# First attention's folded queries: contraction split 128 + 64 instead of 96 + 97 rows, with two heads' 64-row parts on the two halves of the array's rows

## Chip, cores and metric

One core of a Trainium2 chip. The time is the device time of one execution, in microseconds, as the median of the runs.

## What is computed

A post-norm decoder with two layers on x of 4 x 256 tokens and 512 features, all in float32. Each layer is attention, residual, layernorm, feed-forward, residual, layernorm. The change lies in the first layer's attention alone, 32 heads with low-rank queries and keys:

```python
q_c = hidden_size @ Wq_c.T + bq_c                      # 192 features
q = (q_c @ Wq_up.T + bq_up).reshape(b, s, NH, 192).transpose(0, 2, 1, 3)
kv = hidden_size @ Wkv_c.T + bkv_c                     # 64 latent + 64 rope
kv_nope, kv_rope = (kv[..., :64], kv[..., 64:])
kvu = (kv_nope @ Wkv_up.T + bkv_up).reshape(b, s, NH, 256).transpose(0, 2, 1, 3)
k_nope, v = (kvu[..., :128], kvu[..., 128:])
k = jnp.concatenate([k_nope, k_rope], axis=-1)         # k_rope: the same for all heads
scores = jnp.einsum('bhqd,bhkd->bhqk', q, k) / np.sqrt(192)
o = jnp.einsum('bhqk,bhkv->bhqv', softmax(scores), v)
out = jnp.einsum('bhsv,Hv->bsH', o, Wo) + bo           # one Wo for all heads
```

## The kernel before

The kernel never builds q and k of a head. Per head it multiplies the query weights with the key weights first ("the fold"), so that a folded query of 128 features (64 rope, 64 latent) meets the compressed keys kT (128 features x 1024 tokens), which all heads share. A scalar per token and head, beta, comes from the keys' bias; it moves the softmax's maximum. All of this runs before line 330; then come the feed-forward and the second layer, which the change doesn't touch.

The stages of the first attention, in program order:

1. **Projections** (L157 to L171). x transposed comes in four chunks on SyncE's DMA queue, the compressed weights wqc and wkvc on ScalarE's. TensorE makes qcT (192 query features, kept as two slabs of 96 rows, m = 0 and 1; slab 1 has a 97th row of ones, L154, which brings in the biases) and kT. VectorE adds the bias in the copy for qcT, ScalarE for kT. The other weights (wkn, eight groups wqn, the rope rows of wm, wvl, x, ...) follow on SyncE's queue, L138 to L150.
2. **The fold** (L174 to L188). Eight groups of four heads. For each slab m, four matmuls of query weights (96 or 97 columns) against 65 columns of key weights fill a bank ps_o; ScalarE copies slab 0 and VectorE slab 1 into wm, whose innermost index is the head: wm[:, m, :, h] is a strided read. A transpose of kT into cN follows in each group.
3. **First queries and beta** (L192 to L215). q_unit(h, hf) makes the folded queries of one head for 512 tokens: two matmuls (96 rows, then 97) into one bank ps_p, and one ScalarE copy with the scale into qh. Four of these for heads 0 and 1; then beta for eight token tiles, each two matmuls into a bank ps_p and a copy.
4. **The loop** (L298 to L315). j over 16 pairs of heads, b over 4 sequences, one pass for each (j, b). A pass issues scores0(j, b) (scores of two heads into two banks ps_s; maxima, nmb and ebias on VectorE; four exponentials on ScalarE), then, for the pass before, transposes0 (eight transposes into two banks ps_t, and two copies to pT0 and pT1, L269, both on VectorE), one q_unit for the next pair, in passes b = 2 and 3 of some pairs one value_unit (two matmuls into ps_p, added to oacc on VectorE), and output0 (four matmuls of 64 output columns, two heads on the two halves of a bank ps_o). Last, softmax0 normalises on VectorE.
5. **The end** (L316 to L324). The output projection and layernorm.

Banks of PSUM are handed out by tag, L54, with two each for p, s, t and o (L108): a third request of a tag waits until the first one has been read. The framework schedules the instructions at compile time: engines take them in its order, which is not always the order in the text. In the pass shown by the profile VectorE has the first pT copy ahead of nmb, which stands before it in the program.

A matmul of float32 operands is traced as two matmul instructions, each with a weight load of its own (PEld): 128 calls of L64 make 256 rows of ps_p<-qcT,wm.

The lines that decide about waits in the loop:

```python
if todo:
    q_unit(*todo.pop(0))
if flush and b >= 2:
    value_unit(*flush.pop(0))
if pending:
    output0(pending[0], pending[1], pTs)
```

Of the kernel before, what the change touches and what calls it, by code (L numbers as in the profile page):

```python
# [9 lines left out]
F32 = mybir.dt.float32  # L10
I32 = mybir.dt.int32
AF = mybir.ActivationFunctionType
ALU = mybir.AluOpType
# [13 lines left out]
RQ2 = RQ // 2  # L27
I = 1376
NI = -(-I // P)
NI2 = NI // 2  # L30
# [5 lines left out]
QSCALE = 1.0 / math.sqrt(DN + DR)  # L36
# [3 lines left out]
def tile_decoder2(ctx: ExitStack, tc: tile.TileContext, a: dict, out: bass.AP):  # L40
    nc = tc.nc
# [12 lines left out]
    def bank(tag, shape=(P, 512)):  # L54
        return ps["pool"].tile(list(shape), F32, tag=tag, name=f"ps_{tag}", bufs=ps["bufs"][tag])
# [6 lines left out]
    def mm(o, pairs):  # L62
        for i, (l, r) in enumerate(pairs):
            nc.tensor.matmul(o, l, r, start=(i == 0), stop=(i == len(pairs) - 1))  # L64
# [7 lines left out]
        out=mask, in_=mask, pattern=[[0, 2], [-1, P]], compare_op=ALU.is_ge,  # L72
# [4 lines left out]
    xT = const.tile([P, DC, N], F32, name="xT")  # L77
# [27 lines left out]
    NP = NH // 2  # L105
# [1 line left out]
    ps0 = ExitStack()  # L107
    ps0.enter_context(banks("ps0", p=2, s=2, t=2, o=2))  # L108
    with tc.tile_pool(name="l0", bufs=1) as l0, tc.tile_pool(name="l0b", bufs=2) as l0b:
        wkn = l0.tile([P, NH, RKV + 1], F32, name="wkn")  # L110

        wm = l0.tile([RQ2 + 1, 2, P + 1, NH], F32, name="wm")
        wqc = l0.tile([P, DC, RQ], F32, name="wqc")
        wkvc = l0.tile([P, DC, DR + RKV], F32, name="wkvc")
        cb = l0.tile([P, 3], F32, name="cb")
        wvl = l0.tile([P, NP, DV], F32, name="wvl")
        bv = l0.tile([P, NH], F32, name="bv")
        wo0 = l0.tile([P, D], F32, name="wo0")
        bo = l0.tile([P, D], F32, name="bo")
        qcT = l0.tile([RQ2 + 1, 2, N], F32, name="qcT")  # L120
        kT = l0.tile([P, N], F32, name="kT")
        cN = l0.tile([P, NT, RKV], F32, name="cN")

# [12 lines left out]
        nc.scalar.dma_start(out=cb[:RQ2, 0:2], in_=a["bqc"])  # L136
        nc.scalar.dma_start(out=cb[:, 2:3], in_=a["bkvc"])
        nc.sync.dma_start(out=wkn, in_=a["wkn"])  # L138
        wqns = [load_qn(g) for g in range(4)]
        nc.sync.dma_start(out=wm[:RQ2, 0, :DR, :], in_=a["wqr0"])  # L140
        nc.sync.dma_start(out=wm[:RQ2, 1, :DR, :], in_=a["wqr1"][:RQ2])
        nc.sync.dma_start(out=wm[RQ2:, 1, :DR, :], in_=a["wqr1"][RQ2:])
        wqns += [load_qn(g) for g in range(4, NG)]
        nc.sync.dma_start(out=wvl, in_=a["wvl"])
        nc.sync.dma_start(out=bv, in_=a["bv"])
# [4 lines left out]
        nc.sync.dma_start(out=usc, in_=a["usc"])  # L150

        nc.vector.memset(qcT[RQ2:RQ2 + 1, 1, :], 1.0)  # L154
        outs = []
        for hf, tags in enumerate(("pst", "pst")):
            for m in range(3):  # L157
                rows_m = P if m == 2 else RQ2
                outs.append((bank(tags[m]), hf, m, rows_m))
        for c in range(DC):  # L160
            for pj, hf, m, rows_m in outs:
                lhs = wkvc[:, c, :] if m == 2 else wqc[:, c, m * RQ2:(m + 1) * RQ2]
                nc.tensor.matmul(
                    pj[:rows_m], lhs, xT[:, c, bass.ts(hf, 512)], start=(c == 0), stop=(c == DC - 1)
                )
        for pj, hf, m, rows_m in outs:
            cols = bass.ts(hf, 512)
            if m == 2:
                nc.scalar.activation(kT[:, cols], pj, AF.Identity, bias=cb[:, 2:3])
            else:  # L170
                nc.vector.tensor_scalar(qcT[:RQ2, m, cols], pj[:RQ2], cb[:RQ2, m:m + 1], None, ALU.add)  # L171


        for g in range(NG):  # L174
            heads = slice(g * GH, (g + 1) * GH)
            for m in range(2):
                rows_m = RQ2 + m
                pj = bank("o", (P, GH, RKV + 1))
                for hh in range(GH):
                    mm(pj[:rows_m, hh, :], [  # L180
                        (wqns[g][:, hh, m * RQ2:m * RQ2 + rows_m], wkn[:, g * GH + hh, :])
                    ])
                copy = nc.scalar.copy if m == 0 else nc.vector.tensor_copy
                copy(wm[:rows_m, m, DR:, heads], pj[:rows_m].rearrange("p h c -> p c h"))

            tp = bank("t", (P, P))
            nc.tensor.transpose(tp, kT[:, bass.ts(g, P)], ident)
            nc.vector.tensor_copy(cN[:, g, :], tp[:, DR:])  # L188

        qh = {}  # L190

        def q_unit(h, hf):  # L192

            if h not in qh:
                qh[h] = l0b.tile([P, N], F32, tag=f"qh{h % 2}", name=f"qh{h}")
            cols = bass.ts(hf, 512)
            pj = bank("p")
            mm(pj, [
                (wm[:RQ2, 0, :P, h], qcT[:RQ2, 0, cols]),
                (wm[:, 1, :P, h], qcT[:, 1, cols]),  # L200
            ])
            nc.scalar.activation(qh[h][:, cols], pj, AF.Copy, scale=QSCALE)

        for u in [(h, hf) for h in range(2) for hf in range(2)]:
            q_unit(*u)

        beta = l0.tile([P, NT, NH], F32, name="beta")
        for t in range(NT):
            toks = bass.ts(t, P)
            pj = bank("p", (P, NH))  # L210
            mm(pj, [
                (qcT[:RQ2, 0, toks], wm[:RQ2, 0, P, :]),
                (qcT[:, 1, toks], wm[:, 1, P, :]),
            ])
            nc.scalar.activation(beta[:, t, :], pj, AF.Copy, scale=QSCALE)  # L215

        bvs = bv[:, 0:1]
        for n in (16, 8, 4, 2, 1):
# [40 lines left out]
        def transposes0(pr):  # L259
            pTs = []  # L260
            for i in range(2):
                tp = bank("t", (P, 2, S))
                for kt in range(2):
                    for qt in range(2):
                        nc.tensor.transpose(  # L265
                            tp[:, kt, qt * P:(qt + 1) * P], pr[:, i, qt, kt * P:(kt + 1) * P], ident
                        )
                pT = l0b.tile([P, 2, S], F32, tag=f"pT{i}", name=f"pT{i}")
                nc.vector.tensor_copy(pT, tp)  # L269
                pTs.append(pT)  # L270
            return pTs

# [47 lines left out]
        for t in range(NT):  # L320
            pj = bank("p")
# [20 lines left out]
    with tc.tile_pool(name="f0", bufs=1) as f0:  # L342
# [19 lines left out]
        with tc.tile_pool(name="f0i", bufs=2) as f0i, tc.tile_pool(name="f0w", bufs=3) as f0w:  # L362
# [82 lines left out]
            for c in range(NI2):  # L445
# [32 lines left out]
        with tc.tile_pool(name="f0d", bufs=2) as f0d:  # L478
# [78 lines left out]
    with banks("ps1", b0=1, b1=1, b2=1, s=2, t=2, o=1), \  # L557
# [291 lines left out]
        for j in range(NP):  # L849
# [15 lines left out]
            total, at, todo = sum(w for _, w in order), 0, {}  # L865
# [12 lines left out]
            for i in range(2 * B):  # L878
                h, b = (2 * j + i % 2, i // 2) if last else (2 * j + i // B, i % B)
# [5 lines left out]
                if pending:  # L885
                    pT = transposes1(pending[2])
# [11 lines left out]
def _layouts(i):  # L898
# [3 lines left out]
    def chunks(w):  # L902
        return w.reshape(-1, P, w.shape[1]).transpose(1, 0, 2)
# [8 lines left out]
    def columns(s):  # L912
# [3 lines left out]

    i = {k: np.asarray(v) for k, v in i.items()}
    x = i["L0_attn_hidden_size"].reshape(N, D)
    kvc = i["L0_attn_Wkv_c"]
    bkvc = i["L0_attn_bkv_c"]  # L920
# [7 lines left out]
    o = {  # L928
        "x": x.reshape(NT, P, D).transpose(1, 0, 2),
        "xT": chunks(x.T),  # L930
        "wqc": chunks(i["L0_attn_Wq_c"].T),
        "bqc": i["L0_attn_bq_c"].reshape(2, RQ2).T,
        "wkvc": chunks(np.concatenate([kvc[RKV:], kvc[:RKV]], axis=0).T),
        "bkvc": np.concatenate([bkvc[RKV:], bkvc[:RKV]])[:, None],
        "wqn": q[:, :DN].transpose(1, 0, 2),
        "wqr0": qr[:RQ2],
        "wqr1": qr[RQ2:],
        "wkn": kv[:, :DN].transpose(1, 0, 2),
        "wvl": kv[:, DN:, :RKV].reshape(NH // 2, 2, DV, RKV).transpose(1, 3, 0, 2).reshape(P, NH // 2, DV),
        "bv": kv[:, DN:, RKV].T,  # L940
        "wo0": i["L0_attn_Wo"].T,
# [36 lines left out]
```

## Time and profile before

| | us |
|---|---|
| median of 3 runs (lowest, highest) | 1759.63 (1758.41, 1761.05) |
| the profiled execution's own time | 1759.91 |
| its span in the trace | 1758.1 |
| first product of the projections | 4.46 |
| fold begins | 27.53 |
| first queries begin | 39.16 |
| beta and first scores begin | 46.14 |
| first output0 of the loop | 58.41 |
| last pass's output0 | 433.60 |

The granted TensorE clock was full throughout (mean 0.997). In the stretch from 104 to 416 us TensorE is busy for 312.0 of 312 us, VectorE for 220.4, ScalarE for 138.2, GpSimd for nothing, and there is no DMA to speak of. From 4 to 39 us the DMA engines are busy all the time.

How to read it: a row names line, engine, operation, output <- inputs and shape (for a matmul, rows*columns of the weights, then rows x columns of the moving operand). A timeline row gives start, length until the last end, and the number of instructions merged; in brackets the idle time of the engine before it and what ended it. Matmuls are pipelined and their lengths overlap, so start-to-start distances tell what they cost.

### The profile page before, as it was taken

The numbers are of one execution on the slowest core, as the hardware profiler recorded it, in microseconds if no ns is written. First come the engines' busy times: TensorE is split into PE (matmuls) and PEld (weight loads), VectorE is DVE, ScalarE is ACT, GpSimd is POOL, SyncE is SP. The second block draws the span as 40 slices with busy tenths as digits, with TensorE's granted clock in tenths as the row PEclk, the third lists the DMA queues.
The fourth block names the chain that finished last, engine by engine and source line by source line (L and its number), as shares of the span: only waits on it lengthen the run. The fifth ranks groups of instructions, "written<-read, shape, count | busy, mean of one in ns | idle before, by whom it ended". The sixth has DMA issues, their size and how long they took to land.

```text
span 1758.1 us, 20664 instructions
## 1 busy us (share of the span) xinstructions
PE 1722.8 (98%) x7352; PEld 1197.3 (68%) x7352; DVE 1063.8 (61%) x2528; ACT 486.6 (28%) x1584; POOL 478.4 (27%) x502
## 2 busy tenths in 40 slices
PE   8999999999899999999999999999999999999998
PEld 5766666665588885667667767766766776776543
DVE  1677777777745544556656566666656656667644
ACT  1444444444222101122222222222222222222433
POOL 0100000000456434222534335144325315332110
PEclk9999999999999999999999999999999999999999
DMA  8000000000521000101001011011001011010000
GB/s 279 1 1 1 1 1 1 1 1 1 177 70 49 1 1 12 48 25 43 31 24 49 24 36 37 25 36 48 25 24 54 19 49 36 19 48 21 29 12 25
DMA packets 30986, 60.85 MB, mean 35 GB/s; under 512 B 2690, under 2 KB 20354, under 8 KB 29154
## 3 DMA queue, kind: packets, MB, share of 16 engines
q1 hardware_dynamic: 29474, 58.86, 10.6%
q8 instruction: 59, 0.97, 0.2%
q10 hardware_dynamic: 1408, 0.66, 0.1%
q14 instruction: 45, 0.36, 0.1%
HBM read 57.41 MB, written 2.10 MB: 34 GB/s over the span
## 4 chain that ended last, share of the span: by engine, by line
PE 92%; DVE 5%; issue 1%; ACT 1%; DMA 0%; POOL 0%; ACTq 0%; DVEq 0%
PE ps_b L633 20%; PE ps_s L64 12%; PE ps_b L658 11%; PE ps_b L708 9%; PE ps_p L64 9%; PE ps_b L64 4%; PE ps_o L282 4%; PE ps_o L790 3%; PE ps_t L265 3%; PE ps_s L419 3%; PE ps_o L64 3%; PE ps_t L779 2%; PE ps_o L419 2%; PE ps_p L419 2%; PE ps_o L791 2%; DVE pr L773 1%
## 5 line engine op out<-in xcount | busy, mean ns | idle before, releaser
L792 ACT COPY att<-ps_o 128x256 f32<-128x256 f32 x128 | 47.6, 372 | 512.6 <-PE ps_o L791 512.5
L243 ACT ACTIVATE pr<-ps_s,ebias 128x256 f32<-128x256 f32 x256 | 117.7, 471 | 202.6 <-DVE ebias L238 202.6
L763 ACT ACTIVATE pr<-ps_s,nmx 128x128 f32<-128x128 f32 (+1 forms) x256 | 105.4, 417 | 142.2 <-DVE nmx L759 141.4
L716 DVE TENSOR_TENSOR x<-ps_b,x 128x512 f32<-128x512 f32 x168 | 114.9, 687 | 39.3 <-PE ps_b L708 28.9
L726 POOL TENSOR_TENSOR x<-x,po 128x512 f32<-128x512 f32 x84 | 104.8, 1269 | 106.6 <-DVE x L716 78.2
L64 PE MATMUL ps_s<-kT,qh 128*128 128x256 f32 x512 | 130.8, 393 | 0.6 <-ACT pr L243 0.2
L64 PE MATMUL ps_p<-qcT,wm 96*128 96x512 f32 (+1 forms) x256 | 126.5, 618 | 0.0
L373 POOL CAST fwg<-wiwg 128x512 f32<-128x512 int32 (+1 forms) x12 | 7.4, 648 | 403.2 <-DVE st L85 394.2
L64 PEld LDWEIGHTS ps_s<-kT,qh 128*128 128x128 f32 x512 | 90.0, 190 | 35.8 <-ACT pr L243 20.2
L773 DVE TENSOR_SCALAR pr<-pr,rc 128x128 f32<-128x128 f32 (+1 forms) x256 | 110.1, 462 | 4.2
L232 DVE TENSOR_REDUCE nmx<-ps_s 128x2 f32<-128x512 f32 x128 | 88.2, 689 | 37.7 <-PE ps_s L64 35.3
L64 PE MATMUL ps_s<-ck,cq 128*128 128x128 f32 (+1 forms) x512 | 105.2, 328 | 0.0
L755 DVE TENSOR_TENSOR ps_s<-ps_s,mask 128x256 f32<-128x256 f32 x128 | 55.4, 432 | 66.3 <-PE ps_s L64 63.3
L269 DVE COPY pT<-ps_t 128x512 f32<-128x512 f32 x128 | 86.6, 683 | 0.0
L790 PE MATMUL ps_o<-pT,v 128*128 128x256 f32 x256 | 77.4, 384 | 6.5 <-DVE pT L781 4.1
L64 PEld LDWEIGHTS ps_p<-qcT,wm 96*128 96x128 f32 (+1 forms) x256 | 70.9, 299 | 17.6
L759 DVE TENSOR_REDUCE nmx<-ps_s 128x1 f32<-128x128 f32 (+1 forms) x256 | 79.9, 353 | 4.3
L708 PE MATMUL ps_b<-ct,co 128*128 128x256 f32 x336 | 81.9, 380 | 0.0
L254 DVE TENSOR_SCALAR pr<-pr,rc 128x256 f32<-128x256 f32 x256 | 79.1, 349 | 3.1
L779 PEld LDWEIGHTS ps_t<-ident,pr 128*128 128x128 f32 x384 | 49.8, 141 | 41.6 <-issue 34.1
L781 DVE COPY pT<-ps_t 128x384 f32<-128x384 f32 x128 | 70.1, 547 | 12.4 <-PE ps_t L779 12.4
L790 PEld LDWEIGHTS ps_o<-pT,v 128*128 128x128 f32 x256 | 47.4, 190 | 43.3 <-issue 36.0
(248 smaller groups left out, 3559.2 us busy)
## 6 DMA issues: line engine op xcount, KB each, us to landing
w_wa<-in_wq SPq DMA_DIRECT2D x16, 512.0 KB, 3.9
w_wb<-in_wk SPq DMA_DIRECT2D x16, 512.0 KB, 3.9
w_wc<-in_wv SPq DMA_DIRECT2D x8, 1024.0 KB, 5.0
w_wd<-in_wo SPq DMA_DIRECT2D x16, 512.0 KB, 3.8
wqn<-in_wqn SPq DMA_DIRECT2D x8, 386.0 KB, 12.2
wiwg<-in_wg SPq DMA_DIRECT2D x5, 512.0 KB, 3.7
wiwu<-in_wu SPq DMA_DIRECT2D x5, 512.0 KB, 3.6
wid<-in_wd SPq DMA_DIRECT2D x10, 256.0 KB, 2.6
```

Of the source, the lines that this page charges most:

```text
L64: nc.tensor.matmul(o, l, r, start=(i == 0), stop=(i == len(pairs) - 1))
L232: nc.vector.tensor_reduce(nmx[:, i, :], sc, AX.X, ALU.max, negate=True)
L243: nc.scalar.activation(pr[:, i, qt, :], sc[:, qt, :], AF.Exp, bias=bias[:, i, qt:qt + 1], accum_out=sm[:, i, qt:qt + 1],)
L419: nc.tensor.matmul(banks_of[tag], lhs[i][:, k, :], rhs[i][:, k, :], start=first and k == 0, stop=k == 1, skip_group_check=True,)
L633: nc.tensor.matmul(acc, lhs[i][:, k, :], right[i][:, k, :], start=first and k == 0, stop=k == 1, skip_group_check=True,)
L658: nc.tensor.matmul(acc[:, tt, :], right[i][:, k, (t0 + tt) * P:(t0 + tt + 1) * P], lhs[i][:, k, :], start=first and tt == 0 and k == 0, st ...
L708: nc.tensor.matmul(st[tag][:, tt, :], lhs[i][:, (t0 + tt) * P:(t0 + tt + 1) * P], rhs[i], start=first and tt == 0, stop=True, skip_group_c ...
L716: nc.vector.tensor_tensor(xb[m][k], acc, xb[m][k], ALU.add)
L726: nc.gpsimd.tensor_tensor(xb[m][k], xb[m][k], st["p1"], ALU.add)
L763: nc.scalar.activation(pr[:, pt, :], sc[:, pt, :], AF.Exp, bias=nmx[:, qt:qt + 1], accum_out=sm[:, qt:qt + 1],)
L773: nc.vector.tensor_scalar(pr[:, pt, :], pr[:, pt, :], rc[:, qt:qt + 1], None, ALU.mult)
L790: nc.tensor.matmul(po, v[g][:, 2 * b, hv], pT[:, 0:2, :], start=True, stop=False)
```

## The change

The 192 query features are kept as 128 + 64. Slab 0 of qcT holds features 0 to 127; slab 1 holds features 128 to 191 twice, in rows 0 to 63 and again in rows 64 to 127 (wqc has 256 columns now, bqc 128 rows). The folded weights are two tiles: wma, 128 rows for each head, and wmb, whose rows 0 to 63 are the even head's and 64 to 127 the odd head's part, by pairs. The fold fills wmb with matmuls of 64 output columns, the two heads of a pair on the two halves of a bank. The biases are no longer a row of the contraction: the fold makes them in 32 matmuls of 65 weight columns and one moving column (bank pb), and ScalarE adds them, scaled, in the copy out of PSUM (qb). Beta gets a third matmul of one row (crow) and a layout of its own for the 64 rows (wmc, zeros for the other head); all tiles share one bank and one copy, and beta now stands ahead of the first queries.

In the loop, one pass (b = 0, 2) issues the 128-row products of both heads into the two banks ps_p; the next (b = 1, 3) issues the 64-row products, one head on rows 0 to 63 and one on 64 to 127, and then both copies. The second pT copy goes to ScalarE. Value products go to b = 1 and 3 instead of 2 and 3.

```diff
-        wm = l0.tile([RQ2 + 1, 2, P + 1, NH], F32, name="wm")
-        wqc = l0.tile([P, DC, RQ], F32, name="wqc")
+        wma = l0.tile([P, P + 1, NH], F32, name="wma")
+        wmb = l0.tile([P, P + 1, NP], F32, name="wmb")
+        wmc = l0.tile([P, NP, 2], F32, name="wmc")
+        qb = l0.tile([P, NH], F32, name="qb")
+        crow = l0.tile([P, NH + P], F32, name="crow")
+        wqc = l0.tile([P, DC, 2 * P], F32, name="wqc")
...
-        nc.sync.dma_start(out=wm[:RQ2, 0, :DR, :], in_=a["wqr0"])
-        nc.sync.dma_start(out=wm[:RQ2, 1, :DR, :], in_=a["wqr1"][:RQ2])
-        nc.sync.dma_start(out=wm[RQ2:, 1, :DR, :], in_=a["wqr1"][RQ2:])
+        nc.sync.dma_start(out=wma[:, RKV + 1:, :], in_=a["wqra"])
+        nc.sync.dma_start(out=wmb[:, RKV + 1:, :], in_=a["wqrb"])
+        nc.scalar.dma_start(out=qb[RKV:, :], in_=a["bqr"])
...
-        nc.vector.memset(qcT[RQ2:RQ2 + 1, 1, :], 1.0)
+        nc.gpsimd.memset(wmc, 0.0)
+        nc.gpsimd.memset(crow[RKV:RKV + 1, NH:], 1.0)
...
+        pb = bank("p", (P, NH))
         for g in range(NG):
-            heads = slice(g * GH, (g + 1) * GH)
-            for m in range(2):
-                rows_m = RQ2 + m
-                pj = bank("o", (P, GH, RKV + 1))
-                for hh in range(GH):
-                    mm(pj[:rows_m, hh, :], [
-                        (wqns[g][:, hh, m * RQ2:m * RQ2 + rows_m], wkn[:, g * GH + hh, :])
-                    ])
-                copy = nc.scalar.copy if m == 0 else nc.vector.tensor_copy
-                copy(wm[:rows_m, m, DR:, heads], pj[:rows_m].rearrange("p h c -> p c h"))
+            pja = bank("o", (P, GH, RKV + 1))
+            for hh in range(GH):
+                mm(pja[:, hh, :], [(wqns[g][:, hh, :P], wkn[:, g * GH + hh, :RKV + 1])])
+            nc.scalar.copy(wma[:, :RKV + 1, g * GH:(g + 1) * GH], pja.rearrange("p h c -> p c h"))
+            pjb = bank("o", (P, GH // 2, RKV + 1))
+            for hh in range(GH):
+                half = slice((hh % 2) * RKV, (hh % 2 + 1) * RKV)
+                mm(pjb[half, hh // 2, :], [(wqns[g][:, hh, P:RQ], wkn[:, g * GH + hh, :RKV + 1])])
+            pairs = slice(g * GH // 2, (g + 1) * GH // 2)
+            nc.vector.tensor_copy(wmb[:, :RKV + 1, pairs], pjb.rearrange("p h c -> p c h"))
+            for hh in range(GH):
+                h = g * GH + hh
+                mm(pb[:RKV + 1, h:h + 1], [(wkn[:, h, 1:], wqns[g][:, hh, RQ:])])
...
+        for n in range(2):
+            half = slice(n * RKV, (n + 1) * RKV)
+            nc.vector.tensor_copy(wmc[half, :, n], wmb[half, 0, :])
+        nc.scalar.activation(qb[:RKV], pb[:RKV], AF.Copy, scale=QSCALE)
+        nc.scalar.copy(crow[RKV:RKV + 1, :NH], pb[RKV:RKV + 1, :])
+        nc.vector.tensor_scalar(qb[RKV:], qb[RKV:], QSCALE, None, ALU.mult)
...
+        def q_units(j):
...
+            def upper(hf):
+                for n, h in enumerate(heads):
+                    if hf == 0:
+                        qh[h] = l0b.tile([P, N], F32, tag=f"qh{n}", name=f"qh{h}")
+                    acc[n] = bank("p")
+                    nc.tensor.matmul(
+                        acc[n], wma[:, 1:, h], qcT[:, 0, bass.ts(hf, 512)], start=True, stop=False,
+                    )
+
+            def lower(hf):
+                cols = bass.ts(hf, 512)
+                for n, h in enumerate(heads):
+                    half = slice(n * RKV, (n + 1) * RKV)
+                    nc.tensor.matmul(
+                        acc[n], wmb[half, 1:, j], qcT[half, 1, cols], start=False, stop=True,
+                    )
+                for n, h in enumerate(heads):
+                    nc.scalar.activation(
+                        qh[h][:, cols], acc[n], AF.Identity, bias=qb[:, h:h + 1], scale=QSCALE
+                    )
+
+            return [lambda hf=hf, part=part: part(hf) for hf in range(2) for part in (upper, lower)]
...
+        pj = bank("o", (P, NT, NH))
         for t in range(NT):
             toks = bass.ts(t, P)
-            pj = bank("p", (P, NH))
-            mm(pj, [
-                (qcT[:RQ2, 0, toks], wm[:RQ2, 0, P, :]),
-                (qcT[:, 1, toks], wm[:, 1, P, :]),
+            mm(pj[:, t, :], [
+                (qcT[:, 0, toks], wma[:, 0, :]),
+                (qcT[:, 1, toks], wmc.rearrange("p j n -> p (j n)")),
+                (crow[RKV:RKV + 1, NH:], crow[RKV:RKV + 1, :NH]),
             ])
-            nc.scalar.activation(beta[:, t, :], pj, AF.Copy, scale=QSCALE)
+        nc.scalar.activation(beta, pj, AF.Copy, scale=QSCALE)
+        for u in q_units(0):
+            u()
...
-                nc.vector.tensor_copy(pT, tp)
+                (nc.scalar.copy if i else nc.vector.tensor_copy)(pT, tp)
...
-            todo = [(h, hf) for h in (2 * j + 2, 2 * j + 3) for hf in range(2)] if j + 1 < NP else []
+            todo = q_units(j + 1)
...
                 if todo:
-                    q_unit(*todo.pop(0))
-                if flush and b >= 2:
+                    todo.pop(0)()
+                if flush and b % 2:
                     value_unit(*flush.pop(0))
```

More of the change, by code (lines that the diff above doesn't have):

```diff
@@ L26 @@
 RQ, RKV = 192, 64
-RQ2 = RQ // 2
 I = 1376
@@ L109, in tile_decoder2 @@
     with tc.tile_pool(name="l0", bufs=1) as l0, tc.tile_pool(name="l0b", bufs=2) as l0b:
-        wkn = l0.tile([P, NH, RKV + 1], F32, name="wkn")
-        wm = l0.tile([RQ2 + 1, 2, P + 1, NH], F32, name="wm")
-        wqc = l0.tile([P, DC, RQ], F32, name="wqc")
+        wkn = l0.tile([P, NH, RKV + 2], F32, name="wkn")
+        wma = l0.tile([P, P + 1, NH], F32, name="wma")
[4 more added lines that the diff above has]
+        wqc = l0.tile([P, DC, 2 * P], F32, name="wqc")
         wkvc = l0.tile([P, DC, DR + RKV], F32, name="wkvc")
@@ L119, in tile_decoder2 @@
         bo = l0.tile([P, D], F32, name="bo")
-        qcT = l0.tile([RQ2 + 1, 2, N], F32, name="qcT")
+        qcT = l0.tile([P, 2, N], F32, name="qcT")
         kT = l0.tile([P, N], F32, name="kT")
@@ L135, in tile_decoder2 @@
                 nc.sync.dma_start(out=xT[:, c, cols], in_=a["xT"][:, c, cols])
-        nc.scalar.dma_start(out=cb[:RQ2, 0:2], in_=a["bqc"])
+        nc.scalar.dma_start(out=cb[:, 0:2], in_=a["bqc"])
         nc.scalar.dma_start(out=cb[:, 2:3], in_=a["bkvc"])
@@ L150, in tile_decoder2 @@
         nc.sync.dma_start(out=usc, in_=a["usc"])
-        nc.vector.memset(qcT[RQ2:RQ2 + 1, 1, :], 1.0)
[L155 to L159, printed above, removed]
-        for c in range(DC):
[L161 to L166, printed above, removed]
+        nc.gpsimd.memset(wmc, 0.0)
+        nc.gpsimd.memset(crow[RKV:RKV + 1, NH:], 1.0)
+        outs = [(bank("pst"[m]), hf, m) for hf in range(2) for m in range(3)]
+        for c in range(DC):
+            for pj, hf, m in outs:
+                lhs = wkvc[:, c, :] if m == 2 else wqc[:, c, m * P:(m + 1) * P]
+                nc.tensor.matmul(pj, lhs, xT[:, c, bass.ts(hf, 512)], start=(c == 0), stop=(c == DC - 1))
+        for pj, hf, m in outs:
             cols = bass.ts(hf, 512)
@@ L170, in tile_decoder2 @@
             else:
-                nc.vector.tensor_scalar(qcT[:RQ2, m, cols], pj[:RQ2], cb[:RQ2, m:m + 1], None, ALU.add)
+                nc.vector.tensor_scalar(qcT[:, m, cols], pj, cb[:, m:m + 1], None, ALU.add)
+        pb = bank("p", (P, NH))
         for g in range(NG):
-            heads = slice(g * GH, (g + 1) * GH)
-            for m in range(2):
-                rows_m = RQ2 + m
-                pj = bank("o", (P, GH, RKV + 1))
-                for hh in range(GH):
-                    mm(pj[:rows_m, hh, :], [
-                        (wqns[g][:, hh, m * RQ2:m * RQ2 + rows_m], wkn[:, g * GH + hh, :])
-                    ])
-                copy = nc.scalar.copy if m == 0 else nc.vector.tensor_copy
-                copy(wm[:rows_m, m, DR:, heads], pj[:rows_m].rearrange("p h c -> p c h"))
+            pja = bank("o", (P, GH, RKV + 1))
[11 more added lines that the diff above has]
+                mm(pb[:RKV + 1, h:h + 1], [(wkn[:, h, 1:], wqns[g][:, hh, RQ:])])
@@ L186, in tile_decoder2 @@
             tp = bank("t", (P, P))
             nc.tensor.transpose(tp, kT[:, bass.ts(g, P)], ident)
-            nc.vector.tensor_copy(cN[:, g, :], tp[:, DR:])
-        qh = {}
[L192 to L197, printed above, removed]
-            mm(pj, [
[L199 to L202, printed above, removed]
@@ L204, in tile_decoder2 @@
-        for u in [(h, hf) for h in range(2) for hf in range(2)]:
-            q_unit(*u)
+            nc.vector.tensor_copy(cN[:, g, :], tp[:, :RKV])
+        for n in range(2):
[4 more added lines that the diff above has]
+        nc.vector.tensor_scalar(qb[RKV:], qb[RKV:], QSCALE, None, ALU.mult)
@@ new lines, in tile_decoder2 @@
+        qh = {}
+        def q_units(j):
+            if j >= NP:
+                return []
+            heads = (2 * j, 2 * j + 1)
+            acc = {}
+            def upper(hf):
[18 more added lines that the diff above has]
+            return [lambda hf=hf, part=part: part(hf) for hf in range(2) for part in (upper, lower)]
@@ L207, in tile_decoder2 @@
         beta = l0.tile([P, NT, NH], F32, name="beta")
+        pj = bank("o", (P, NT, NH))
         for t in range(NT):
             toks = bass.ts(t, P)
-            pj = bank("p", (P, NH))
-            mm(pj, [
-                (qcT[:RQ2, 0, toks], wm[:RQ2, 0, P, :]),
-                (qcT[:, 1, toks], wm[:, 1, P, :]),
-            ])
-            nc.scalar.activation(beta[:, t, :], pj, AF.Copy, scale=QSCALE)
+            mm(pj[:, t, :], [
+                (qcT[:, 0, toks], wma[:, 0, :]),
+                (qcT[:, 1, toks], wmc.rearrange("p j n -> p (j n)")),
+                (crow[RKV:RKV + 1, NH:], crow[RKV:RKV + 1, :NH]),
+            ])
@@ L918, in _layouts @@
     x = i["L0_attn_hidden_size"].reshape(N, D)
-    kvc = i["L0_attn_Wkv_c"]
-    bkvc = i["L0_attn_bkv_c"]
+    wqc = i["L0_attn_Wq_c"]
+    bqc = i["L0_attn_bq_c"]
     q = np.concatenate([i["L0_attn_Wq_up"], i["L0_attn_bq_up"][:, None]], axis=1)
@@ L930, in _layouts @@
         "xT": chunks(x.T),
[L931 to L934, printed above, removed]
+        "wqc": chunks(np.concatenate([wqc, wqc[P:]], axis=0).T),
+        "bqc": np.concatenate([bqc, bqc[P:]]).reshape(2, P).T,
+        "wkvc": chunks(i["L0_attn_Wkv_c"].T),
+        "bkvc": i["L0_attn_bkv_c"][:, None],
         "wqn": q[:, :DN].transpose(1, 0, 2),
-        "wqr0": qr[:RQ2],
-        "wqr1": qr[RQ2:],
-        "wkn": kv[:, :DN].transpose(1, 0, 2),
+        "wqra": qr[:P],
+        "wqrb": np.concatenate([qr[P:RQ, :, 0::2], qr[P:RQ, :, 1::2]], axis=0),
+        "bqr": qr[RQ],
+        "wkn": np.concatenate([kv[:, :DN, RKV:], kv[:, :DN]], axis=2).transpose(1, 0, 2),
         "wvl": kv[:, DN:, :RKV].reshape(NH // 2, 2, DV, RKV).transpose(1, 3, 0, 2).reshape(P, NH // 2, DV),
```

## The prediction

> **What bounds the kernel now.** First the page: TensorE has no idle time to speak of, and it carries the chain that ends last. The products that the change rewrites are the ps_p row, 256 instructions of one pass each.
>
> ```profile
> PE 1722.8 (98%) x7352; PEld 1197.3 (68%) x7352; DVE 1063.8 (61%) x2528; ACT 486.6 (28%) x1584; POOL 478.4 (27%) x502
> ...
> PE 92%; DVE 5%; issue 1%; ACT 1%; DMA 0%; POOL 0%; ACTq 0%; DVEq 0%
> ...
> L64 PE MATMUL ps_p<-qcT,wm 96*128 96x512 f32 (+1 forms) x256 | 126.5, 618 | 0.0
> ```
>
> Then TensorE's timeline over one pass of the inner loop (start, length, then the instructions merged). Lengths overlap, so I read starts.
>
> ```profile
> 171.89 1.99 PE L64 MATMUL ps_p<-qcT,wm 96*128 96x512 f32 x4
> 173.80 1.08 PE L282 MATMUL ps_o<-pT,cN 128*64 128x256 f32 x8
> 174.82 2.00 PE L64 MATMUL ps_s<-kT,qh 128*128 128x256 f32 x8
> 176.65 1.04 PE L265 MATMUL ps_t<-ident,pr 128*128 128x128 f32 x8
> 177.52 0.70 PE L64 MATMUL ps_p<-qcT,wm 96*128 96x512 f32 x1
> ```
>
> Start to start: queries 1.91, output 1.02, scores 1.83, transposes 0.87, together 5.63 us. Eight score instructions of 256 columns need 2.00 - 0.38 (length of the last) = 1.62 for seven steps, so one step is about 0.215 us, and 0.43 for 512 columns. In the output row eight instructions lie within 1.08: 1.08 - 0.38 = 0.70 is three steps. So they start two at a time, from the first: 64-column products on two halves of the array run together.
>
> Third, DVE and ACT over the same pass, and the end of the loop, where no queries are left to compute:
>
> ```profile
> 171.83 0.68 DVE L269 COPY pT<-ps_t 128x512 f32<-128x512 f32 x1
> 172.42 0.15 DVE L236 TENSOR_TENSOR nmb<-nmx,beta 128x4 f32<-128x4 f32 x1
> 172.49 0.69 DVE L269 COPY pT<-ps_t 128x512 f32<-128x512 f32 x1
> 173.09 0.16 DVE L238 TENSOR_TENSOR ebias<-nmb,beta 128x4 f32<-128x4 f32 x1
> ```
>
> ```profile
> 422.58 1.61 PE L282 MATMUL ps_o<-pT,cN 128*64 128x256 f32 x8
> 427.95 1.75 PE L282 MATMUL ps_o<-pT,cN 128*64 128x256 f32 x8 [0.65 <-DVE pT L269]
> ```
>
> ```profile
> 173.37 0.47 ACT L243 ACTIVATE pr<-ps_s,ebias 128x256 f32<-128x256 f32 x1 [3.69 <-DVE ebias L238]
> ```
>
> The exponentials wait for ebias, and ebias sits behind the second pT copy. There the period is 427.95 - 422.58 = 5.37: the loop through DVE and ACT. So a pass is bound by TensorE (5.63) with the softmax loop 0.26 behind it. Shorter queries alone would gain little; ACT's 3.69 idle is room for a copy.
>
> **The change part by part, against the profiled execution** (span 1758.1; its own time 1759.91; the median of the runs is 1759.63, 0.3 less).
>
> *Queries in the loop.* For two heads and 512 tokens there were 8 instructions in two passes of the loop, 4 and 4. Now the even pass has 4 with 128 rows (same 0.43 steps: no change), the odd pass has 4 of 64 rows, two for each half. If halves of the rows pair as halves of the columns do, these are two steps, 0.86. To this comes the change of tile mode. The Trainium skill (TensorEngine Tiling, Tiling Modes, Key Properties) says that changing the mode drains TensorE, which speaks against this change; it gives no time. The trace does: the four query steps from 171.89 end at 171.89 + 0.10 (first weights) + 4 x 0.43 = 173.71, and the output starts at 173.80, 0.09 late; and its first weights, no longer loaded ahead, add 0.05. Here the weights are 128 columns:
>
> ```profile
> L64 PEld LDWEIGHTS ps_s<-kT,qh 128*128 128x128 f32 x512 | 90.0, 190 | 35.8 <-ACT pr L243 20.2 <-issue 5.4
> L64 PEld LDWEIGHTS ps_p<-qcT,wm 96*128 96x128 f32 x128 | 33.3, 305 | 0.8
> L282 PEld LDWEIGHTS ps_o<-pT,cN 128*64 128x64 f32 x512 | 32.0, 136 | 55.5 <-DVE ebias L238 29.6 <-DVE pr L254 6.1 <-DVE rc L252 5.3
> ```
>
> From 64 to 128 packed columns a load grows 54 ns, 0.85 a column; strided by heads (305) it is about 115 more, some 0.22 us exposed. So the odd pass is 0.09 + 0.22 + 0.86 + 0.09 (drain before the output) = 1.26 instead of 1.91: 0.65 less. By the rule without the row I would have no number; with no drain it would be 1.05 less. 15 pairs of heads x 2 = 30 such passes: -19.6.
>
> What is late next? With the second pT copy on ACT, ebias follows nmb at once, 0.6 earlier, so the softmax loop is about 4.8, under the odd pass's 5.63 - 0.65 = 4.98. Its copy (about 0.6, by the 606 ns eviction of the same size) falls in ACT's 3.69 idle and costs nothing; with that cover gone it would delay four exponentials. ACT's two evictions in the odd pass (1.2 instead of 0.6) have the same cover. The last pair of heads, bound by the softmax loop at 5.37, gains 0.5 in four passes: -2.0.
>
> *Value products* go to odd passes, behind the lower products. Both ps_p banks then wait for ACT's evictions, which queue behind the four exponentials; behind the value product on TensorE are the output and the next scores. 14 places. Between nothing (the scheduler puts output and the first scores ahead) and 1.25 (the value product first: output done 1.0 after the lower products, bank free some 2.3 after). The trace shows work that is ready put ahead of work that isn't (the pT copy before nmb), so I take 0.15: +2.
>
> *Fold.* A group takes 28.98 - 27.53 = 1.45 now, of it 0.11 the transpose, so 0.084 for each of 16 loads of 96 columns:
>
> ```profile
> 27.53 1.50 PE L64 MATMUL ps_o<-wkn,wqn 128*96 128x65 f32 x16
> 28.87 0.28 PE L187 MATMUL ps_t<-ident,kT 128*128 128x128 f32 x1
> 28.98 1.50 PE L64 MATMUL ps_o<-wkn,wqn 128*96 128x65 f32 x16
> ```
>
> After: 8 loads of 128 columns at 0.111 = 0.89; 8 on column halves, four steps of 0.06, with 0.14 in and 0.16 out = 0.54; 8 for the bias, 65 weight columns for one moving column. For these the skill's floor per matmul (TensorE: Matmul & The Clock Gate, Back-to-back issue gap: about 25 ns however few columns) would give 0.2; but the row says that loads set the pace, 0.058 each: 0.41. Transpose 0.11. Sum 1.95, +0.5 x 8 = +4.0 (3 to 6).
>
> *Beta.* Per token tile 4 instructions of 0.111, now 2 more with one row, in another tile mode: 0.09 + 0.21 + 0.10 out = +0.40, x 8 = +3.2 (0.22 x 8 = 1.8 with no drain, 4.5 with the longer loads). Beta also goes ahead of the queries, so the first softmax no longer has beta products to cover it: a bubble of about +0.9 (scores' end to first bank free 2.7, covered by 1.8 of queries). The first pair's queries save 2 x 0.65: -1.3.
>
> *At nothing:* memsets, the small copies and the qb load (beside the fold's TensorE work; uncovered under 0.5 each); the loads behind wqn, whose issue order on SP stays. The 0.13 MB more of wqc delay the first product by about +0.1.
>
> Sum: -19.6 - 2.0 + 2.0 + 4.0 + 3.2 + 0.9 - 1.3 + 0.1 = -12.7. 1759.63 - 12.7 = **1747**.
>
> **Rivals.**
> - *Row halves start in strict order.* The skill (same page, Part 3, What overlaps and what doesn't) says that matmuls start in order. If both passes of a head stand before the other head's, three steps instead of two: 0.43 back in 32 places, +13.8: about 1760.5. The output row speaks against it (three steps to the last start, not four), but those are column halves; no row of the trace shows row halves.
> - *Row halves don't overlap at all* (slower). Four steps: +0.86 x 32 = +27.5: 1774.5. It decides from the point where the overlap saves less than 14.8 / 32 = 0.46 of the 0.86 per place, for without it the change costs 1774.5 - 1759.6 = 14.8. For it: no row of the trace has products on row halves. Against: column halves pair from the first step, and the two heads write different banks.
> - *Overlap as forecast, but the moved waits bite:* value products stall 1.25 in 14 places (+15.5 beyond mine), or the ACT copy lands behind the exponentials in some passes: about 1762. Against: ready work is put ahead.
>
> **How the numbers follow.** Forecast 0.54 (own range 1739 to 1754: fold and beta at their bounds, value stalls 0 to 6, and the 0.12 by which 22 passes run at 5.75 instead of 5.63, -2.6 if they even out); strict order 0.14; no overlap 0.17; waits 0.15. A measurement tells 0.2%, 3.5 us, from no change: faster is below 1756.1, slower above 1763.2. Faster: 0.54, 0.02 of strict order and 0.03 of waits: 0.59. Same: 0.10 of strict order and 0.03 of waits: 0.13. Slower: the rest, 0.28. The range 1739 to 1774 leaves out half of no overlap and the far ends of the others.
>
> **What would show it.** Right: the four 64-row instructions start two at a time, so that their row in the timeline is about 0.43 long to the last start; even passes 5.63, odd about 5.0; pT's second copy ahead of the exponentials on ACT; fold groups near 1.95. Wrong: the same row at 0.86 or 1.3 to the last start; TensorE waiting for ACT qh in odd passes; odd passes over 5.4.

## The result, and the profile after

| | before | after |
|---|---|---|
| median of 5 runs (lowest, highest) | 1759.63 (1758.41, 1761.05) | 1771.89 (1765.65, 1773.13) |
| ratio, with its 95% interval | | 1.0057 (1.0035 to 1.008) |
| span of the profiled execution | 1758.1 | 1771.3 |
| fold begins | 27.53 | 27.49 |
| first scores begin | 46.51 | 75.18 |
| first output0 of the loop | 58.41 | 83.94 |
| first product of the output projection | 435.14 | 445.85 |
| second layer's first product | 673.99 | 686.66 |

The kernel became slower, by 12 us; the forecast was 13 us faster. Of its five runs three took 1771.9 to 1773.1 us, with a mean clock of 0.984, and two 1765.7 us, with 0.988 and 0.989; the profile is that of the longest. The loop did get faster: from the first output0 to the output projection it took 376.7 us and takes 361.9, 14.8 less. All of that and more had been lost ahead of it: the loop starts 25.5 us late. The page of the changed kernel, with the lines that answer to those shown of before and the row of the clock:

```profile
PE 1733.0 (98%) x7432; PEld 1201.1 (68%) x7432; DVE 1033.5 (58%) x2466; ACT 531.5 (30%) x1643; POOL 478.5 (27%) x504
...
PEclk8699999999999999999999999999999999999999
...
PE 90%; DVE 6%; ACT 2%; issue 1%; DMA 0%; POOL 0%; ACTq 0%; DVEq 0%
```

TensorE is as busy as it was, and the chain is still its own. What is new are two digits: in the first two fortieths of the span (to 44 and to 89 us) the granted clock was 0.8 and 0.6. In the kernel before that row has a 9 in every place. (Its clock was not full quite throughout: from 671.49 to 678.32 us, after an idle stretch between the two layers, it was half, and every kernel here has such a dip.) The same by stretches (length, then busy time and instructions of each engine, the granted clock, the DMA share and GB/s):

```profile
core 0: us, PE busy (x) PEld busy (x) DVE busy (x) ACT busy (x) POOL busy (x), PEclk, DMA share, GB/s
...
27.00:32.77 5.77, 5.77 (x69) 5.19 (x68) 1.84 (x6) 1.44 (x3) 0.00 (x0) 1.00 1.06 432
32.77:49.00 16.23, 16.23 (x119) 15.16 (x118) 2.30 (x9) 2.16 (x7) 10.84 (x13) 0.50 0.26 99
49.00:55.00 6.00, 6.00 (x26) 3.93 (x25) 0.93 (x4) 0.47 (x2) 0.00 (x0) 0.50 0.00 0
55.00:68.00 13.00, 13.00 (x51) 11.62 (x51) 0.00 (x0) 0.28 (x1) 0.00 (x0) 0.50 0.00 0
```

From 32.77 to 73.73 us, that is in nearly all of the fold, in beta and in the first queries, TensorE ran at half clock, although from 32.77 to 49.00 us it was busy for 16.23 of 16.23 us, and before the drop for 5.77 of 5.77. A fold group takes 3.85 us there and a token tile of beta 1.55. Then the clock is full again, and the loop shows the mechanism that was forecast. TensorE's timeline over an odd pass and the start of one with a value product:

```profile
175.69 1.04 PE L295 MATMUL ps_t<-ident,pr 128*128 128x128 f32 x8
176.66 1.23 PE L223 MATMUL ps_p<-qcT,wmb 64*128 64x512 f32 x4
177.82 1.08 PE L312 MATMUL ps_o<-pT,cN 128*64 128x256 f32 x8
178.84 1.13 PE L63 MATMUL ps_s<-kT,qh 128*128 128x256 f32 x4
180.05 1.98 PE L63 MATMUL ps_p<-pc,wvl 128*128 128x512 f32 x4
181.87 1.03 PE L63 MATMUL ps_s<-kT,qh 128*128 128x256 f32 x4
```

The four 64-row instructions lie within 1.23; one of them is 0.59 long, so the last starts 0.64 after the first: 0.43 for one step and 0.21 for weights. They start two at a time. From output0 to output0, behind the first eight passes, even passes take 5.63 to 5.64 us and odd ones 4.98. Passes with a value product take 7.70: the four score steps before it are through at 178.84 + 4 x 0.215 = 179.70, but it starts at 180.05, because its bank is still being read. VectorE and ScalarE in that odd pass:

```profile
177.29 0.16 DVE L268 TENSOR_TENSOR ebias<-nmb,beta 128x4 f32<-128x4 f32 x1
177.49 0.47 ACT L273 ACTIVATE pr<-ps_s,ebias 128x256 f32<-128x256 f32 x1
...
179.30 1.28 ACT L227 ACTIVATE qh<-ps_p,qb 128x512 f32<-128x512 f32 x2
```

The exponential starts as soon as ebias is there, and both evictions of queries stand behind the four exponentials.

### The profile page after: what moved, and what is told of

The parts are those of the page before. It is cut to its first block, busy times and chain, and to the rows that moved or that the text cites. A ratio compares the mean times of both kernels' runs of the same rounds, so it can differ in the third digit from the quotient of the medians.

```text
span 1771.3 us, 20814 instructions
## 1 busy us (share of the span) xinstructions
PE 1733.0 (98%) x7432; PEld 1201.1 (68%) x7432; DVE 1033.5 (58%) x2466; ACT 531.5 (30%) x1643; POOL 478.5 (27%) x504
## 4 chain that ended last, share of the span: by engine, by line
PE 90%; DVE 6%; ACT 2%; issue 1%; DMA 0%; POOL 0%; ACTq 0%; DVEq 0%
PE ps_b L663 20%; PE ps_s L63 11%; PE ps_b L688 11%; PE ps_b L738 9%; PE ps_o L63 4%; PE ps_b L63 4%; PE ps_p L215 4%; PE ps_o L820 3%; PE ps_o L312 3%; PE ps_s L449 3%; PE ps_p L63 3%; PE ps_t L295 2%; PE ps_t L809 2%; PE ps_o L449 2%; PE ps_p L449 2%; PE ps_p L223 2%
## 5 line engine op out<-in xcount | busy, mean ns | idle before, releaser
L299 ACT COPY pT<-ps_t 128x512 f32<-128x512 f32 x64 | 37.5, 586 | 144.5 <-PE ps_t L295 144.5
L809 PEld LDWEIGHTS ps_t<-ident,pr 128*128 128x128 f32 x384 | 49.8, 141 | 41.7 <-issue 34.1
L801 DVE RECIPROCAL rc<-sm 128x2 f32<-128x2 f32 x128 | 20.6, 162 | 87.8 <-ACT pr L793 87.5
L312 PE MATMUL ps_o<-pT,cN 128*64 128x256 f32 x512 | 70.1, 392 | 1.4 <-ACT pT L299 0.7
```

Source lines behind the costliest of these rows:

```text
L312: nc.tensor.matmul(po[i * RKV:(i + 1) * RKV, :], cN[:, 2 * b + kt, :], pTs[i][:, kt, :], start=(kt == 0), stop=(kt == 1),)
```

## Experiments

**Theory:** the fold and beta of the changed kernel feed TensorE so few moving columns per microsecond that its clock is halved; the work itself costs what was forecast. **Rival:** the fold and beta are simply long (narrow products, changes of tile mode, loads of weights), and the clock is beside the point. To compare stages I count a *streaming share*: the columns of the matmul instructions that start in a window, times 0.83 ns (a 512-column step takes 0.43 us), over the window; two products on halves count twice. I worked it out from the starts in the trace, in which some records are missing, so a difference of 0.01 or 0.02 means little. The window is 3.41 us, because stretches at half clock are 3.41 us long or a multiple of it: 40.96 here, and 13.65, 17.07 and 20.48 below.

In the window before the drop, 29.36 to 32.77, the share was 0.43, without any idle time: the schedule put the bias products (one moving column each) of two groups close together there. The kernel before has 0.67 to 0.74 in its fold.

**e1_mix: wide products among the narrow ones, the same work.** Half of the projections' products (512 columns) are held back and issued one or two ahead of each fold group, the transposes of kT come after the fold, and beta is made two tiles at a time in the loop's first four passes.

```diff
+        later = [(c, *o) for c in range(DC) for o in outs[3:]]
...
         for g in range(NG):
+            for _ in range(2 - g % 2):
+                project(*later.pop(0))
             pja = bank("o", (P, GH, RKV + 1))
...
+                if j == 0:
+                    beta_unit(b)
                 pr, sm = scores0(j, b)
```

> The changed kernel with the same instructions in another order: the second half of the projections (512 columns each) is put between the groups of the fold, the transposes of kT after them, and beta's products are spread over the first four passes of the loop. Theory (clock): the granted TensorE clock fell to half from 32.8 to 73.7 us because one window of 3.4 us had matmuls streaming for only 0.43 of it; mixed with wide products no window falls under 0.5, the clock stays whole, and about 20 us come back: 1749 to 1754. Rival (work): the fold's and beta's own instructions and mode changes are the loss; their number is the same, so 1768 to 1774.

Measured: 1751.64 us, ratio 0.9953 (0.9941 to 0.9966). The clock stays full through the whole attention; the first output0 comes at 64.72 instead of 83.94. The same products in another order, 20 us less: the rival falls.

**e2_no_bias: the changed kernel without its 32 bias products.**

```diff
+        nc.vector.memset(pb, 0.0)
...
-            for hh in range(GH):
-                h = g * GH + hh
-                mm(pb[:RKV + 1, h:h + 1], [(wkn[:, h, 1:], wqns[g][:, hh, RQ:])])
```

> The changed kernel without the 32 bias products of the fold (the folded queries' bias from the up-projection is left out, zeros stand in its place). Theory (clock): without them a group of the fold streams about 0.59 of its time, so the clock survives the fold; it then falls in beta's eight tiles (0.2 of their time) and comes back with the first queries, so the half clock lasts 10 to 15 us instead of 41: 1753 to 1758. Rival (work): only the 32 products' own 3.5 to 4 us are saved: about 1768.

Measured: 1757.14 us, ratio 0.9984 (0.9976 to 0.9992). The fold, now with shares of 0.61 to 0.77, keeps its clock. Beta loses it, after a window with a share of 0.19, for 13.65 us (45.84 to 59.49). In that window (42.42 to 45.84) TensorE also stands idle, in beta's first tile, until VectorE has copied wmc:

```profile
45.03 0.38 PE L63 MATMUL ps_o<-wmc,qcT 128*128 128x32 f32 x2 [1.22 <-DVE wmc L193]
```

So this run doesn't show that beta's thin products would have been enough without the wait.

**e3_beta_spread: the changed kernel with only beta spread over the first four passes** (the last two added lines of e1_mix).

> The changed kernel with beta's products spread over the first four passes of the loop, the fold as it is. Theory (clock): the fold alone trips the clock at the same place, near 32.8 us; without beta's 12 us of sparse products behind it the first queries bring it back near 57 to 60 us instead of 73.7, so about 8 to 10 us are saved: 1762 to 1765. Rival (beta is the cause): the clock does not fall in the fold: under 1757.

Measured: 1758.29 us, ratio 0.9989 (0.9983 to 0.9996), less than expected. The drop comes in the fold, but later (columns as in the stretches above; the clock is the third figure from the right):

```profile
34.35:37.76 3.41, 3.41 (x44) 3.27 (x43) 0.86 (x4) 0.38 (x1) 0.00 (x0) 1.00 0.62 225
37.76:54.83 17.07, 16.80 (x88) 11.75 (x86) 2.19 (x9) 2.06 (x7) 9.84 (x8) 0.50 0.01 2
```

Until then the fold's products stand in the same order and at the same distances as in the changed kernel (the second group's bias products 1.95 us behind the fold's start in both); what differs is where the windows fall. The first one that lies whole in the fold starts 1.87 us behind its start in the changed kernel, 2.85 here. Windows with 0.51 and 0.48 kept the clock, the one with 0.45, busy for 3.41 of 3.41 us, lost it. So the fold suffices to lose the clock without beta, and when it does depends on the place of the windows. That may also be why the changed kernel's own runs fall into two groups; only one of them was profiled.

**e8_more_work: the changed kernel in its own order, with 16 unread products of 512 columns added.** In each fold group and for each token tile of beta:

```diff
+            sp = bank("s")
+            nc.tensor.matmul(sp, kT[:, :P], kT[:, :512], start=True, stop=True)
```

> The changed kernel, order as it is, with 16 products added that nobody reads (kT against kT, 128 columns of weights, 512 moving columns): one in each fold group and one for each token tile of beta. They cost 16 x 0.86 = 13.8 us at full clock. If it is sparse streaming that costs the changed kernel its clock, the fold and beta stay at full clock, and the 20 us of half clock go: 1763 to 1768, less time for more work. If the fold and beta are long by their own work and not by the clock: 1783 to 1787.

Measured: 1768.24 us, ratio 1.0046 (1.0033 to 1.0058): some 3.7 less than the changed kernel's median, though the intervals overlap and two of that kernel's five runs took less. It is 0.2 above the first range, and the total doesn't decide; the stretches of fold and beta do:

```profile
core 0: us, PE busy (x) PEld busy (x) DVE busy (x) ACT busy (x) POOL busy (x), PEclk, DMA share, GB/s
...
28.00:51.00 23.00, 23.00 (x218) 17.69 (x217) 4.31 (x18) 4.07 (x11) 10.86 (x13) 1.00 0.38 153
51.00:65.00 14.00, 14.00 (x66) 9.52 (x65) 0.23 (x1) 0.12 (x1) 0.00 (x0) 1.00 0.00 0
```

The clock is full in both, and the first output0 comes at 80.79 instead of 83.94, with 15 us more work ahead of it. (The added products also keep the bias products of two groups apart.) This run also gives the price of the fold without the clock (TensorE's timeline; the row of two is the added product):

```profile
27.95 1.38 PE L63 MATMUL ps_o<-wkn,wqn 128*128 128x65 f32 x16
29.27 0.63 PE L63 MATMUL ps_p<-wqn,wkn 128*65 128x1 f32 x8
29.76 1.10 PE L191 MATMUL ps_s<-kT 128*128 128x512 f32 x2
30.70 0.27 PE L193 MATMUL ps_t<-ident,kT 128*128 128x128 f32 x1
30.81 1.39 PE L63 MATMUL ps_o<-wkn,wqn 128*128 128x65 f32 x16
```

A group is 30.81 - 27.95 = 2.86, of it 30.70 - 29.76 = 0.94 added: 1.92. The forecast was 1.95. In the same way a tile of beta is 0.79 (1.755 less 0.97), against 0.44 before; in e3_beta_spread, with no wide product between, it is 0.90 (58.56 to 59.46).

**e9_beta_320 and e10_beta_192: the dose.** As e8, with 256 columns in each fold group and 320 or 192 for each tile of beta.

```diff
+            sp = bank("s")
+            nc.tensor.matmul(sp[:, :256], kT[:, :P], kT[:, :256], start=True, stop=True)
...
+            sp = bank("s")
+            nc.tensor.matmul(sp[:, :320], kT[:, :P], kT[:, :320], start=True, stop=True)
```

> Dose of added products: the changed kernel with an unread product of 256 moving columns in each fold group and one of 320 columns for each token tile of beta (with 16 of 512 columns it took 1768.2 at full clock). The added work is 8 x 0.43 + 8 x 0.53 = 7.7 us instead of 13.8. Share of a window in which columns stream: 0.62 in the fold, (0.16 + 0.53) / 1.42 = 0.49 in beta. If the clock holds above about 0.47: full clock throughout, 1761 to 1764. If it needs more than that: half clock in beta, 1768 to 1771.

> As the run with 320 columns, but 192 for each token tile of beta: 1.7 us less work, and a share of (0.16 + 0.32) / 1.21 = 0.40 in beta. If the share of streaming decides, with its bound between 0.43 and 0.47: full clock in the fold, half clock from beta's second window on for some 10 to 14 us, 1765 to 1768, so more time than with 320 columns although it does less. If the share doesn't decide: 1759 to 1762, 1.7 us less than with 320.

Measured: 1763.12 us (ratio 1.0025, 1.0014 to 1.0036) with 320 columns, 1765.82 (1.0036, 1.0023 to 1.0048) with 192. The intervals of the two ratios overlap, but beta's stretch differs, first in e9_beta_320:

```profile
46.00:58.00 12.00, 11.88 (x70) 9.81 (x68) 1.64 (x3) 0.37 (x2) 1.29 (x2) 1.00 0.00 0
```

and in e10_beta_192:

```profile
46.00:58.00 12.00, 10.76 (x45) 10.00 (x44) 2.14 (x3) 0.14 (x1) 1.89 (x2) 0.61 0.00 0
```

With a share of 0.48 to 0.52 beta keeps the clock; with one of 0.30 in its first whole window it loses it, for 20.48 us. But that window (45.27 to 48.68) has a wait for wmc in it, where TensorE is idle for 1.24 us (in e9_beta_320 for 0.12). The row is that of e10_beta_192:

```profile
48.07 0.38 PE L63 MATMUL ps_o<-wmc,qcT 128*128 128x32 f32 x2 [1.24 <-DVE wmc L197]
```

The two runs thus differ in idle time as well as in columns (0.40 was expected without the wait), and they don't show the dose by itself. With 320 columns two of the 14 runs took 1772 us, with a mean clock of 0.990 in place of 0.996.

**e4_pt_act_alone: the kernel before, with only the second pT copy on ScalarE.**

```diff
-                nc.vector.tensor_copy(pT, tp)
+                (nc.scalar.copy if i else nc.vector.tensor_copy)(pT, tp)
```

> The kernel before with one part of the change alone: the second pT copy on ScalarE. Theory: the loop is bound by TensorE at 5.63 a pass, so the copy alone gains only where the softmax loop binds (the last pair, about 2) and where the early order costs 0.12 a pass (up to 2.6): 1755 to 1759. Rival (the softmax loop is the bound and the query halves give nothing): 1745 to 1750.

Measured: 1755.13 us, ratio 0.9975 (0.9967 to 0.9984). The passes of 5.75 become 5.63, and the last pair's five passes take 23.4 instead of 25.6.

**e6_pt_on_vector: e1_mix with this copy back on VectorE** (the same edit reversed).

> The mixed kernel (e1) with the second pT copy back on VectorE. If the softmax loop of 5.37 then bounds the odd passes, these take 5.37 instead of 4.98 (30 x 0.39 = +11.7) and the last pair's passes 5.37 instead of 4.8 (+2): some 1764 to 1767. If the copy's move matters only as in the kernel before (there it gave 4.5 us alone): 1755 to 1757.

Measured: 1782.8 us, ratio 1.0128 (1.0114 to 1.0142): 31 more than e1_mix, and neither expectation. Eight passes take 49.8 instead of 46.6, and the first eight 57.2, of it 1.9 for a value product that falls into them, instead of 46.0. VectorE and ScalarE in a later one:

```profile
180.84 0.15 DVE L281 TENSOR_TENSOR ebias<-nmb,beta 128x4 f32<-128x4 f32 x1
181.00 0.69 ACT L237 ACTIVATE qh<-ps_p,qb 128x512 f32<-128x512 f32 x1 [3.32 <-PE ps_p L233]
181.58 0.47 ACT L286 ACTIVATE pr<-ps_s,ebias 128x256 f32<-128x256 f32 x1
```

With ebias late, an eviction of queries stands ahead of the exponentials, and the softmax loop becomes longer than the 5.37 that I had put in. In the first eight passes there is a second cause, some 9 of the 31 us: the order puts other products between the two heads' 64-row products, so that they don't pair. In the rest they pair, and there the copy's place is worth more than alone (4.5): it keeps the exponentials ahead of the evictions.

**e5_one_half: e1_mix with both heads' 64-row products on the same half of the rows.**

```diff
-                        acc[n], wmb[half, 1:, j], qcT[half, 1, cols], start=False, stop=True,
+                        acc[n], wmb[:RKV, 1:, j], qcT[:RKV, 1, cols], start=False, stop=True,
```

> The mixed kernel (e1), but the 64-row products of both heads lie on rows 0 to 63 of the array (the odd head's queries are then built from the even head's rows: wrong values, same work). If the pairing of the row halves is what the loop gains, the four 64-row instructions of an odd pass take four steps instead of two: +0.86 in 30 passes of the loop, odd passes 5.84 instead of 4.98, some +26 us over the mixed kernel's 1751.6: 1775 to 1779. If the halves only fall beside other work and their pairing is worth little (the softmax loop of 4.8 just behind), well under that: 1755 to 1765.

Measured: 1771.5 us, ratio 1.0065 (1.005 to 1.008), 19.9 more than e1_mix. Four steps instead of two:

```profile
174.71 2.09 PE L233 MATMUL ps_p<-qcT,wmb 64*128 64x512 f32 x4
176.72 1.08 PE L325 MATMUL ps_o<-pT,cN 128*64 128x256 f32 x8
```

Odd passes take 5.83 instead of 4.98, 30 x 0.85 = 25.5. That the sum is less has a cause, too: passes with a value product take 7.35 here and 7.70 in e1_mix, 14 x 0.35 = 4.9. With the longer odd pass the banks are read in time: ScalarE starts on them at 177.34, and the value product starts without a gap at 178.70.

**e7_value_even: e1_mix with the value products in even passes, ahead of the transposes.**

```diff
                 pr, sm = scores0(j, b)
+                if flush and b % 2 == 0:
+                    value_unit(*flush.pop(0))
                 if pending:
...
-                if flush and b % 2:
-                    value_unit(*flush.pop(0))
```

> The mixed kernel (e1) with the value products in even passes (b = 0 and 2), ahead of the transposes, when both p banks have been read. If the value products stall on the evictions of the 64-row products (7.70 measured against 7.35 for a pass with value products), this saves 0.35 in 14 places and more: 1745 to 1748. If the stall only moves (the 128-row products then wait for VectorE's read of the value bank): 1750 to 1755. The dip of the clock in the feed-forward part may move or go (1.8 us), since it comes later by a fraction of a window.

Measured: 1745.22 us, ratio 0.9918 (0.9904 to 0.9932): faster than both kernels. The value product starts without a gap:

```profile
191.66 1.99 PE L63 MATMUL ps_s<-kT,qh 128*128 128x256 f32 x8
193.49 1.88 PE L63 MATMUL ps_p<-pc,wvl 128*128 128x512 f32 x4
195.21 1.04 PE L308 MATMUL ps_t<-ident,pr 128*128 128x128 f32 x8
```

Its passes take 7.35, and from the first output0 to the output projection the kernel needs 355.8 us instead of e1_mix's 360.6. The two profiled executions differ by 8.0 us; 1.2 of it lies ahead of the first output0, and 2.0 is the clock: e1_mix has a window at half clock in the feed-forward part (564.97 to 568.38), this one none, and that part takes 238.6 instead of 240.6.

## Why the prediction was wrong

| step | forecast | measured |
|---|---|---|
| fold, group | 1.95 (+4.0) | 1.92 at full clock (+3.8); 3.85 at half clock |
| beta, tile | +0.40 (+3.2) | +0.34 (+2.7) in e8_more_work, +0.46 in e3_beta_spread, at full clock; 1.55 in all at half clock |
| first pair's queries | -1.3 | +0.3 (e8_more_work) |
| until the first output0 | +6.9 | about +7.2 at full clock; +25.5 in the changed kernel |
| odd pass | 4.98 | 4.98, in all but the first eight passes |
| first eight passes, without value products | -2.6 | +1.4 |
| value stall, each of 14 | 0.15 | 0.35 (13 of them) |
| passes of 5.75 even out | range only (-2.6) | -2.1 behind the first eight (e4_pt_act_alone) |
| last pair | -2.0 | -2.2 (e4_pt_act_alone) |
| loop, first output0 to output projection | -19.6 | -14.8 |

**The step that failed** is the pair "Fold" and "Beta": it priced their instructions by rows that had been recorded at full clock, and took for granted that the clock would stay; no rival named the clock either. The instructions were sized well: take the added products (8 x 0.94 + 0.86 + 7 x 0.97 = 15.2) out of e8_more_work's 80.79 and the first output0 would come at 65.6, 7.2 later than before. That the sum came so close to 6.9 is in part luck: fold and beta came out lower, and the first pair's queries saved nothing (64.77 to 72.03 in e8_more_work, 7.3 us instead of 7.0), because their second half waits 0.82 us for ScalarE to read the banks. The bias products were also summed short: eight at 0.058 are 0.46, not 0.41; they measured 0.49. By the same subtraction the changed kernel at full clock would have had a span of 1765.5 - 15.2 = 1750.3, 7.8 less than before (an estimate; e1_mix, with the clock kept in the attention, has 1750.3 as measured). Half clock then costs the profiled execution 1771.3 - 1750.3 = 21.0: 18.3 ahead of the loop and 1.6 in the feed-forward part; the last 1.1 lies in the second layer, which varies by as much between these kernels. In the feed-forward part 582.31 to 585.73 is a window with a share of 0.31, in which TensorE waits 2.3 us for VectorE's hT, and the next one ran at half clock; in the kernel before, the same wait is split between two windows of 0.56 and 0.69.

What would have warned: the share can be worked out before the change is built. A fold group has 16 x 65 + 2 x 128 columns or so, 1.08 us of streaming: 0.74 of 1.45 before, 0.55 of 1.95 after, and less where the bias products of two groups come together. A tile of beta streams 0.16 of some 0.8 us; before it was half as long, and its 3.6 us lay next to queries and scores in the same windows (0.52 to 0.63). The trace of before didn't show where the bound lies: its lowest busy window, 0.52, kept the clock, and 0.55 for the fold is above that. Beta's 0.2 was far below any busy window of it. I checked the mean clock of the kernel before, and didn't ask what held it.

**The loop** fell short by 4.8. The value stall was 0.2 larger in 13 of the 14 places (+2.6; the mechanism, an eviction behind the exponentials, was the one named). In the first eight passes the compile-time order put scores between the two heads' 64-row products, so that they couldn't pair: odd passes of 6.13, and 49.4 us for the eight, of it 1.9 for a value product that fell into them, against 46.1 before (+1.4 instead of -2.6). Both are of the order, not of the array: e7_value_even and e1_mix are free of the one and the other. The evened passes gave 2.1 back: 4.0 + 2.6 - 2.1 is 4.5.

**The rivals.** Strict order and no overlap are wrong: the starts show pairs (0.64 us from the first of the four to the last), and e5_one_half shows what no overlap costs, 0.85 a pass. "Moved waits" was right in kind, with 0.35 in place of 1.25. None of them was the reason for the slower time; the measured 1771.9 lies near "no overlap" (1774.5), and inside the range of 1739 to 1774, by coincidence.

## What to carry to other kernels

When a change makes products narrower or adds small ones, work out how many columns stream per microsecond in that stage, window by window, not only how long the instructions are: a TensorE that issues without a pause can lose half its clock, and the price is then the whole stage, not the added work. Where a stage is sparse, issue wide products among the narrow ones, or spread the narrow ones over a dense loop; it costs nothing in work. And where two products are meant to run on two halves of the array, look in the trace whether the order still has them next to each other.

## What was not expected of the hardware

- A busy TensorE loses its clock. Of the windows in which it was never idle, those with a share of 0.43 (the changed kernel) and 0.45 (e3_beta_spread) were followed by half clock, and those with 0.47 and 0.48 (e3_beta_spread, e9_beta_320) and more were not; 0.02 is within what the count can miss. Weighting each product by the rows and columns of the array it fills doesn't order these windows (in e3_beta_spread 0.35 kept it, 0.38 lost it).
- Where a window also has idle time, the share orders less well. 0.19 (e2_no_bias), 0.30 (e10_beta_192) and 0.31 (the changed kernel) lost the clock, 0.41 and 0.44 (e7_value_even) kept it; but 0.37 lost it in e9_beta_320's feed-forward part, with 1.9 us idle, and kept it near 449 us in the same trace, with 1.7 idle. What is counted there stays open.
- The Trainium skill (TensorE: Matmul & The Clock Gate, Part 1: The HAM clock gate) ties the half rate to an idle window and the full rate to a busy one, in windows of 3.41 us. The length agrees with the multiples here, the idle window doesn't: the changed kernel was busy for 5.77 of 5.77 us ahead of the drop, and then for 16.23 of 16.23 us at 0.50.
- Being busy doesn't bring the clock back either. One window below the bound was followed by twelve at half clock (40.96 us). At half clock 512 columns take 0.86 us, so a TensorE full of wide products streams a share of 0.50 there. Windows with 0.38 and 0.41 (the changed kernel) and 0.44 (e3_beta_spread) didn't bring it back; it came after windows with 0.50 and more. One with 0.52, part of it two halves at once and part of it a wait (66.91 to 70.32 in the changed kernel), didn't. One bound for losing and regaining the clock, in columns per microsecond, would fit nearly all of this; no run here was made to test it.
- At half clock the steps on TensorE take about twice as long: a fold group 3.85 instead of 1.92, a tile of beta 1.55 instead of 0.79. A load of 128x128 weights in the fold is recorded with 335 ns instead of 193.
- The two passes of a float32 product on one half pair with those on the other half: the four start at 0, 0.01, 0.64 and 0.64 us. In the kernel's text one head's product stands first; in which order the four were issued the trace doesn't show.
